# Row sums of the 8-wide squares on TensorE at places 4, 13 and 14 of a period of sixteen

## The chip, the cores and the metric

The kernel runs on one core of one Trainium2 chip. The metric is the device time of one execution in microseconds. The engines are named as in the profile: PE (TensorE, with PEld for its weight loads), DVE (VectorE), ACT (ScalarE), POOL (GpSimd) and SP (SyncE, which here only issues DMAs). Each engine works through its own queue of instructions in order, and the order of PE, DVE, ACT and POOL is fixed when the kernel is written.

## The reference

The input x has 8 batches of 512 tokens of 256 numbers. Four layers follow each other, each added to x after a layer norm: attention A, a feed-forward block, attention B, and the same feed-forward block again. Attention A is the unusual one. It projects each token to 16 heads of 64 channels, and attends *between the channels of one head of one token*:

```
Q = (x @ Wq + bq).reshape(b, s, 16, 64) / 8        # K and V alike, without the 1/8
scores = einsum('bshq,bshk->bshqk', Q, K)          # 64 x 64 for each token and head
w = softmax(where(k > q, -inf, scores))            # causal in the channels
out = x + einsum('bshqk,bshk->bshq', w, V).reshape(b, s, 1024) @ Wo + bo
```

For each q this needs two row sums over k <= q: of exp(q k), the denominator, and of exp(q k) v, the numerator. The feed-forward block has two gate products, two hidden layers of 1024 x 1024 and an output product. Attention B is an ordinary causal attention over 512 tokens with 16 heads.

## The kernel before

**Tiles.** Attention A works on tiles of 128 tokens (the partitions) and 4 heads (256 columns). Batch b has 16 such tiles: group g of heads (0 to 3, the outer loop) and token tile i (0 to 3). Tile number n = 16b + 4g + i, and *the place* of a tile is n mod 16; sixteen tiles make a period. So place 4 is g = 1, i = 0; place 13 is g = 3, i = 1; place 14 is g = 3, i = 2.

**Squares.** The triangle k < q of a head is cut into one square of 32, two of 16, four of 8, and so on down to 1; the diagonal is added apart (`acc`, line 834). Each square is an outer product of rows q and columns k, and its row sums are wanted. A tile has four units (`units`): unit 0 and unit 2 (the 32-squares of two heads each), unit 1 (the 16-squares), and unit 3 (all squares of 8, 4, 2 and 1, tile `ws`, two halves of 1920 columns: exp, and exp times v). A unit runs through these steps:

- `scores` (L855): the products q k, units 0 to 2 on POOL in two instructions each, unit 3 on DVE in four;
- `exps` (L878) on ACT;
- `weigh` (L890): times v, on DVE;
- `halve` (L897), units 0 to 2: a DMA issued by POOL adds one half of `w` to the other in place (accumulate, 1 MB);
- the sums of what is left. Unit 0 by PE: `sums32` (L918) turns 16 blocks of 128 columns into one accumulating PSUM block, `keep_sums` (L980, ACT) copies it, `turn_sums` (L989, PE) turns it back, `add32` (L1000, DVE) adds it to `acc`. Unit 2: a POOL add (`fold`, L905) and a DVE reduction; unit 1: a DVE reduction. Unit 3: `gather` (L1047) reduces the squares of 8 and of 4 on DVE into `red` tiles, `small_squares` (L1023, L1063) does those of 2 and 1 on POOL, and `adds` (L1063) adds the `red` tiles to `acc` on POOL;
- `invert` (L1069, DVE), `divide` (L1075, POOL), `turn_group` (L1085, PE), `keep_att` (L1089, ACT), `project_out` (L1101, PE) and `new_x` (L1114, ACT) finish the tile.

The PSUM tile `bank` has two halves. Half 1 serves only `sums32` (first 128 columns) and `turn_sums` (the other 128); half 0 serves the projections of a tile (L803), the turned x (L621), `turn_group` and `project_out`. `take` and `free` check when the kernel is built that no two uses overlap.

**Order.** A tile has a new slot every 1/12 of a tile period. The table `order` gives each step a slot relative to its tile (step `gather 3` at slot 18 of tile n stands in the same slot as step 6 of tile n + 1), and `slot()` (line 741) issues what falls on a slot in the table's own order. The first batch has a table of its own (`first`). Attention A of batch b runs beside the later layers of batch b - 1, which are written as one generator (`after_a`):

```
while spent * 12 * NT * NG < total * (at + 1 - 12 * NT * NG - 33):
    spent += next(done)
```

Each step of that generator is worth some units (`pace` times a number), and `total` is the worth of one batch. So the hidden layers (L1365 on PE, L1326 and L1327 on ACT, L1331 on DVE), the gate (L1293 on PE, L1268 and L1276 on ACT, L1272 and L1277 on DVE) and attention B (L1444, L1511, L1523) stand at fixed places between the steps of attention A: in batch 3 the hidden layers of one feed-forward block run between the reciprocals of places 2 and 6, attention B between those of 6 and 11, the gate of the other block between those of 11 and 13, and its hidden layers from there to the end of the period.

Of the kernel before, what the change touches and what calls it, by code (L numbers as in the profile page):

```python
# [9 lines left out]
F32 = mybir.dt.float32  # L10
# [33 lines left out]
 'p16': 2,  # L44
 'rot': 4,
 'half': [0, 0, 0, 0, 1, 1],
 'order': [[8, 'scores', 2, 1, 2], [10, 'exps', 2], [22, 'small_squares'], [20, 'add16'], [-120, 'load'],
           [-26, 'normalise'], [6, 'exps', 1], [13, 'sums32', 0], [23, 'adds', 3], [32, 'turn_group'],
           [22, 'keep_sums', 2], [16, 'keep16'], [9, 'weigh', 1], [-1, 'scores', 0, 0, 2], [11, 'fold', 0],
           [12, 'turn16'], [6, 'halve', 0], [11, 'scores', 3, 0, 1], [-30, 'ahead'], [14, 'sums16'],  # L50
           [22, 'add32', 2], [12, 'weigh', 2], [21, 'turn_sums', 2], [34, 'project_out'],
           [4, 'scores', 1, 1, 2], [-8, 'project'], [10, 'halve', 1], [36, 'new_x'], [25, 'divide'],
           [13, 'weigh', 3], [7, 'scores', 2, 0, 2], [15, 'turn_sums', 0], [17, 'fold', 2], [32, 'keep_att'],
           [-5, 'keep_qk'], [12, 'halve', 2], [13, 'keep_sums', 0], [18, 'add32', 0], [18, 'gather', 3],
           [-22, 'turn_x'], [24, 'invert'], [13, 'gather', 1], [16, 'adds', 1], [20, 'sums32', 2],
           [12, 'exps', 3], [4, 'weigh', 0], [3, 'exps', 0], [1, 'scores', 1, 0, 2], [-22, 'keep_x'],
           [0, 'scores', 0, 1, 2]],
 'first': {'sum': ['pe16', 'pe16'],
           'p16': 2,
           'sum16': 'dve',  # L60
           'order': [[21, 'small_squares'], [23, 'adds', 3], [21, 'sums32', 2], [-23, 'turn_x'],
                     [29, 'divide'], [0, 'scores', 0, 1, 2], [4, 'scores', 1, 0, 2], [15, 'turn16'],
                     [26, 'invert'], [19, 'add32', 0], [6, 'scores', 2, 0, 2], [6, 'halve', 0],
                     [-1, 'scores', 0, 0, 2], [-27, 'normalise'], [9, 'fold', 0], [7, 'exps', 1],
                     [10, 'exps', 2], [20, 'gather', 3], [15, 'turn_sums', 0], [4, 'weigh', 0],
                     [23, 'turn_sums', 2], [15, 'weigh', 3], [-120, 'load'], [-30, 'ahead'], [16, 'keep16'],
                     [10, 'scores', 3, 0, 1], [-21, 'keep_x'], [17, 'adds', 1], [19, 'sums16'],
                     [23, 'add32', 2], [8, 'weigh', 1], [10, 'halve', 1], [36, 'new_x'],
                     [4, 'scores', 1, 1, 2], [13, 'weigh', 2], [-5, 'keep_qk'], [6, 'scores', 2, 1, 2],
                     [14, 'exps', 3], [31, 'turn_group'], [21, 'add16'], [21, 'keep_sums', 2],  # L70
                     [15, 'gather', 1], [32, 'keep_att'], [13, 'fold', 2], [14, 'sums32', 0],
                     [14, 'keep_sums', 0], [-8, 'project'], [34, 'project_out'], [13, 'halve', 2],
                     [2, 'exps', 0]],
           'on': ['adds0']},
 'sum16': 'dve',
 'lo': 'psum',
 'pace': {'gate': 1.8, 'attn': 0.65, 'wait': 1.354, 'w3': 1.05, 'out': 0.95, 'turn': 0.997},
 'total': 304.842,
 'eps': 'dve',
 'U': {'wait': 14.4,  # L80
       'gate': 33.0,
# [3 lines left out]
       'out': 5.6,  # L85
       'qk': 13.6,
       'attn': 72,
       'proj': 21}}


@with_exitstack
# [241 lines left out]
def fast_path(ctx: ExitStack, tc: tile.TileContext, k, t, flag):  # L333
# [216 lines left out]
    def bank_half(j):  # L550
        return bank[:, j, :]
# [85 lines left out]

    JB = 8

    def kind(b, n_u):  # L640
        c = G["first"] if b == 0 and "first" in G else G
        return c["sum"][n_u // 2] if n_u in (0, 2) else c.get("sum16", "dve")

    def reds(b):
        return (G["first"] if b == 0 and "first" in G else G).get("red", [])

    def on(b):
        return (G["first"] if b == 0 and "first" in G else G).get("on", [])

    def p16(b):  # L650
        return (G["first"] if b == 0 and "first" in G else G)["p16"]

    def by_columns(b, n_u):
        return n_u < 3 and kind(b, n_u) != "dve"
# [1 line left out]
    def pieces(w, n, off, nsq, cols, b, n_u, parts):  # L656
# [4 lines left out]
        def of_cols(v):  # L661
            return v[:, cols].rearrange("p (x t) -> p x t", t=2 * n)[:, :, :n]

        if n < 16:
            e, ev = (
                w[:, a * SMALL + off : a * SMALL + off + nsq * n * n].rearrange("p (x i j) -> p x i j", i=n, j=n)
                for a in range(2)
            )
            yield e, ev, lambda v: of_rows(v).unsqueeze(3), lambda v: of_cols(v).unsqueeze(2)
        elif by_columns(b, n_u):  # L670
            both = w.rearrange("p (j a x i) -> p a j x i", a=2, x=nsq, i=n)
            step = n // parts
            for k in range(0, n, step):
                yield (
                    both[:, 0, k : k + step],
                    both[:, 1, k : k + step],
                    lambda v: of_rows(v).unsqueeze(1),
                    lambda v, k=k: of_cols(v)[:, :, k : k + step].rearrange("p x j -> p j x").unsqueeze(3),
                )
        elif n == 32:  # L680
            both = w.rearrange("p (b a x i j) -> p a b x i j", a=2, x=nsq, i=n, j=JB)
            for x in range(nsq):
                yield (
                    both[:, 0, :, x],
                    both[:, 1, :, x],
                    lambda v, x=x: of_rows(v)[:, x].unsqueeze(1).unsqueeze(3),
                    lambda v, x=x: of_cols(v)[:, x].rearrange("p (b j) -> p b j", j=JB).unsqueeze(2),
                )
        else:
            both = w.rearrange("p (b a x i j) -> p a b x i j", a=2, x=nsq, i=n, j=JB)  # L690
            for k in range(n // JB):
                yield (
                    both[:, 0, k],
                    both[:, 1, k],
                    lambda v: of_rows(v).unsqueeze(3),
                    lambda v, k=k: of_cols(v)[:, :, k * JB : (k + 1) * JB].unsqueeze(2),
                )
# [10 lines left out]
    class AttentionA:  # L708
# [32 lines left out]
        def slot(self, t):  # L741

            now = []
            for lo, hi, order in TABLES:
                for place, (slot, what, args) in enumerate(order):
                    late = 8 if what in ("normalise", "turn_x", "keep_x") and t - slot in (12, 20) else 0
                    n, r = divmod(t - slot - late, 12)
                    if r == 0 and lo <= n < hi and (late == 0 or t - slot == 20):
                        now.append((place / len(order), what, self.todo[n] + args))
            for _, what, args in sorted(now, key=lambda p: p[0]):  # L750
                getattr(self, what)(*args)

        def take(self, h, *cells):
# [175 lines left out]
        def sums16(self, b, i, g):  # L929
# [1 line left out]
            if kind(b, 1) == "dve": return  # L931
            assert (b, i, g, 1, "h") in self.seen
            w = self.live.pop((b, i, g, 1)).rearrange("p (j r) -> p j r", r=2 * P)
            self.take(1, 0, 1)
            for r in range(2):
                for j in range(8):
                    nc.tensor.matmul(
                        bank_half(1)[:, r * P : (r + 1) * P], w[:, j, r * P : (r + 1) * P], ident,
                        start=(j == 0 and r == 0), stop=(j == 7), is_transpose=True, skip_group_check=True,
                    )  # L940
            assert "fwd" not in self.live
# [2 lines left out]
        def keep16(self, b, i, g):  # L944
# [1 line left out]
            if kind(b, 1) == "dve": return  # L946
            assert self.live.pop("fwd") == (b, i, g, 1)
            self.live["sums16"] = ap_.tile([P, 2 * P], F32, tag="red128", name="sums16", bufs=3)
            nc.scalar.copy(self.live["sums16"], bank_half(1))
            self.free(1, 0, 1)  # L950

        def turn16(self, b, i, g):

# [1 line left out]
            assert "back" not in self.live  # L955
            self.live["back"] = (b, i, g, 1)
            s16 = self.live.pop("sums16")
            self.take(1, 0, 1)
            for r in range(2):
                nc.tensor.transpose(bank_half(1)[:, r * P : (r + 1) * P], s16[:, r * P : (r + 1) * P], ident)  # L960

        def add16(self, b, i, g):

            if kind(b, 1) == "dve": return
# [1 line left out]
            acc = self.live[b, i, g][2]  # L966
            rows = acc.rearrange("p a (x t) -> p a x t", t=32)[..., 16:]
            nc.vector.tensor_tensor(
                rows, rows, bank_half(1).rearrange("p (a x i) -> p a x i", a=2, i=16), ALU.add
            )  # L970
            assert (b, i, g, 0, "w") in self.seen
            self.free(1, 0, 1)
            self.done[b, i, g] += 1

        def keep_sums(self, b, i, g, n_u):
# [38 lines left out]
        def small_squares(self, b, i, g):  # L1014
# [4 lines left out]
            for n, off, nsq, cols in squares(units[NU - 1]):  # L1019
                if n <= 2 and n not in reds(b):  # L1020
# [1 line left out]
                    if n == 2:  # L1022
                        (nc.vector if "small" in on(b) else nc.gpsimd).tensor_tensor(both[..., :1], both[..., :1], both[..., 1:], ALU.add)  # L1023
                    self.add_rows(b, i, g, n, cols, both[..., 0], "small")
            if (b, i, g, NU - 1, "r") in self.seen: self.live.pop((b, i, g, NU - 1))

        def gather(self, b, i, g, n_u):

# [1 line left out]
            assert (b, i, g, n_u, "h" if n_u < NU - 1 else "w") in self.seen  # L1030
            self.seen.add((b, i, g, n_u, "r"))
            w = self.live[b, i, g, n_u]
            if n_u < NU - 1 or (b, i, g, n_u, "s") in self.seen: self.live.pop((b, i, g, n_u))
            self.sums[b, i, g, n_u] = []
            here = 0
            for n, off, nsq, cols in sorted(squares(units[n_u]), key=lambda u: u[0] in reds(b)):
                if n in reds(b):
                    assert all((b, i, g, k, what) in self.seen for k in range(NU) for what in "pew")
                    red = self.live[b, i, g][0][:, here % 2].rearrange("p (a r) -> p a r", a=2)
# [719 lines left out]
```

## Time and profile before

| | us |
|---|---|
| three runs | 3621.72, 3622.65, 3628.54 (median 3622.65) |
| the profiled execution | 3620.43, of which the span of its instructions is 3618.6 |
| DVE busy | 3124.0 (86%) |
| PE busy | 3048.9 (84%) |
| POOL busy | 2971.8 (82%) |
| ACT busy | 2505.2 (69%) |
| first and last reciprocal of attention A (L1069) | at 53.2 and 3328.6 |

A reciprocal ends the sums of a tile, so its 128 starts mark the tiles. Batch 0, which runs alone, takes 337.9 us from its first reciprocal to that of batch 1; the six periods after it take 422.8, 422.0, 420.1, 425.0, 426.6 and 424.3 us; after the last reciprocal 290 us follow in which the later layers of batch 7 run alone. A row of a group of instructions reads: line, engine, operation, tiles and shapes, count | busy us, mean ns of one | idle time of the engine just before them, and what ended it. In the timeline the number in square brackets is the idle time of the engine before that instruction and what released it. A row of a window reads: stretch, its length, then PE, PEld, DVE, ACT and POOL busy us with counts, the clock granted to PE (1.00 is full), the DMA share and GB/s.

### The profile page before, as it was taken

The page shows a single profiled execution, that of the slowest core. Times are in us where ns is not written, and L with a number is a line of the kernel's source. Part 1 is how long each engine was busy: PE and PEld are TensorE (multiplying, and loading weights), DVE is VectorE, ACT ScalarE, POOL GpSimd, SP SyncE. Part 2 cuts the span into 40 slices and gives each one's busy share as a digit, 9 for nine tenths or more (in the row PEclk, how much of TensorE's full clock was granted, in tenths as well). Part 3 has the DMA queues.
Part 4 walks back from the last instruction along what each step waited for, and adds up shares of the span by engine and source line. Part 5 has one row for each costly group of instructions (what it writes and reads, how often), then busy time and mean ns, then how long its engine had stood idle before and what let it go on. Part 6 is the DMA issues. An engine that isn't in the chain of part 4 may idle for free.

```text
span 3618.6 us, 42449 instructions
## 1 busy us (share of the span) xinstructions
PE 3048.9 (84%) x14468; PEld 2168.6 (60%) x14468; DVE 3124.0 (86%) x3844; ACT 2505.2 (69%) x3488; POOL 2971.8 (82%) x2682
## 2 busy tenths in 40 slices
PE   7765698798887998888987988879888889878998
PEld 4544475476645766466754766457664667556756
DVE  7999998999889998999988998899989998896227
ACT  4544686687767787687866877668866878665453
POOL 7999988888898989989898888989889888885000
PEclk8878799898998999998998989989999999989999
DMA  9978897688877988689876888769877788767414
GB/s 240 200 160 165 178 228 163 149 215 194 206 165 167 231 206 185 141 204 213 224 167 144 217 191 204 167 155 232 195 190 150 193 208 209 175 146 221 131 53 170
DMA packets 117038, 665.34 MB, mean 184 GB/s; under 512 B 12742, under 2 KB 30665, under 8 KB 43467
## 3 DMA queue, kind: packets, MB, share of 16 engines
q0 software_dynamic: 80640, 587.24, 71.1%
q1 hardware_dynamic: 35896, 75.02, 6.0%
q8 instruction: 116, 1.90, 0.2%
q14 instruction: 110, 0.90, 0.1%
q10 hardware_dynamic: 276, 0.27, 0.0%
HBM read 251.18 MB, written 8.65 MB: 72 GB/s over the span
## 4 chain that ended last, share of the span: by engine, by line
PE 33%; DVE 22%; POOL 17%; ACT 14%; issue 9%; DMA 5%; ACTq 0%; POOLq 0%; SPq 0%; DVEq 0%
POOL w L855 8%; PE ph L1365 8%; DVE w L890 6%; DVE red L1047 5%; DMA w<-w 5%; PE pw L1293 4%; POOL acc L1063 3%; PE pyb L1523 3%; ACT w L878 3%; DVE ws L855 3%; PE pqkb L1444 3%; PE bank L918 3%; PE psb L1511 2%; POOL w L897 2%; PE qv L808 2%
## 5 line engine op out<-in xcount | busy, mean ns | idle before, releaser
L855 POOL TENSOR_TENSOR w<-k 128x1024 f32<-128x1024 f32 x768 | 1617.6, 2194 | 44.2 <-DVE red L1047 23.0
L1365 PE MATMUL ph<-h,hidden 128*128 128x512 f32 x4096 | 1019.6, 403 | 6.5 <-DVE h L1277 2.4
L890 DVE TENSOR_TENSOR w<-w,qv 128x1024 f32<-128x1024 f32 (+1 forms) x624 | 890.2, 1458 | 83.9 <-ACT w L878 83.8
L1365 PEld LDWEIGHTS ph<-h,hidden 128*128 128x128 f32 x4096 | 766.4, 190 | 186.7 <-issue 21.0
L878 ACT ACTIVATE w<-w 128x2048 f32<-128x2048 f32 x384 | 734.6, 1915 | 138.5 <-POOL w L855 136.5
L897 POOL DMA_DIRECT2D w<-w x384 | 352.3, 918 | 193.3 <-DVE w L890 94.7
L1293 PE MATMUL pw<-xnt,gate 128*128 128x512 f32 (+2 forms) x1152 | 346.4, 452 | 153.4 <-ACT silu L1268 99.3
L1047 DVE TENSOR_REDUCE red<-w 128x256 f32<-128x2048 f32 x240 | 426.8, 1778 | 23.7 <-DMA w<-w 22.0
L1047 DVE TENSOR_REDUCE red<-ws 128x256 f32<-128x2048 f32 (+1 forms) x256 | 435.6, 1742 | 0.0
L1063 POOL TENSOR_TENSOR acc<-acc,red 128x256 f32<-128x256 f32 x496 | 392.1, 791 | 29.5 <-DVE red L1047 11.0
L1293 PEld LDWEIGHTS pw<-xnt,gate 128*128 128x128 f32 x1152 | 236.3, 225 | 242.1 <-ACT silu L1268 124.0
L918 PE MATMUL bank<-ident,w 128*128 128x128 f32 x2304 | 322.6, 301 | 52.1 <-ACT x L1114 26.4
L855 DVE TENSOR_TENSOR ws<-qv,k 128x1024 f32<-128x1024 f32 (+3 forms) x512 | 300.0, 647 | 76.9 <-POOL acc L1063 76.8
L918 PEld LDWEIGHTS bank<-ident,w 128*128 128x128 f32 x2304 | 298.3, 158 | 80.0 <-ACT x L1114 39.2
L890 DVE TENSOR_TENSOR ws<-ws,qv 128x1024 f32<-128x1024 f32 (+3 forms) x512 | 294.9, 636 | 32.0 <-ACT ws L878 32.0
L905 POOL TENSOR_TENSOR w<-w 128x1024 f32<-128x1024 f32 x112 | 280.2, 2502 | 50.7 <-DMA w<-w 50.6
L808 PE MATMUL qv<-wqv,xnta 128*128 128x512 f32 x512 | 269.9, 653 | 27.3 <-DVE ws L890 22.0
L878 ACT ACTIVATE ws<-ws 128x1920 f32<-128x1920 f32 x128 | 233.1, 1821 | 76.2 <-DVE ws L855 72.6
L1331 DVE TENSOR_TENSOR h<-ph,h 128x512 fp32r<-128x512 f32 x256 | 167.8, 681 | 90.3 <-ACT ph L1327 84.1
L1518 ACT ACTIVATE eb<-psb 128x512 f32<-128x512 f32 (+3 forms) x503 | 181.9, 459 | 89.2 <-PE psb L1515 88.9
L1326 ACT ACTIVATE h<-ph,s_sb 128x512 fp32r<-128x512 f32 x256 | 176.6, 690 | 94.2 <-PE ph L1365 92.2
L1069 DVE RECIPROCAL acc<-acc 128x256 f32<-128x256 f32 x128 | 223.1, 1743 | 3.9 <-POOL acc L1063 3.9
(163 smaller groups left out, 4867.5 us busy)
## 6 DMA issues: line engine op xcount, KB each, us to landing
w<-w POOLq DMA_DIRECT2D x384, 1024.0 KB, 7.6
hidden<-in_h POOLq DMA_DIRECT2D x128, 1024.0 KB, 6.4
gate<-in_w12p POOLq DMA_DIRECT2D x32, 1024.0 KB, 6.7
w<-in_w3p POOLq DMA_DIRECT2D x16, 1024.0 KB, 6.0
wqv<-wqv_d SPq DMA_DIRECT2D x31, 512.0 KB, 3.9
wo<-in_wo SPq DMA_DIRECT2D x32, 256.0 KB, 7.4
w<-in_h SPq DMA_DIRECT2D x8, 1024.0 KB, 6.9
wk<-wk_d SPq DMA_DIRECT2D x31, 256.0 KB, 6.2
```

Of the source, the lines that this page charges most:

```text
L808: nc.tensor.matmul(qv.rearrange("p j f -> p (j f)"), xnt[:, c, :], wqv[:, c, :], start=(c == 0), stop=(c == DC - 1),)
L855: eng.tensor_tensor(e, rows(q).to_broadcast(shape), columns(kt[:, 0]).to_broadcast(shape), ALU.mult)
L878: nc.scalar.activation(e, e, AF.Exp, scale=C**-0.5)
L890: nc.vector.tensor_tensor(ev, e, columns(qv[:, 1]).to_broadcast(list(e.shape)), ALU.mult)
L897: nc.gpsimd.dma_start(w[:, :2048], w[:, 2048:], accum_op=ALU.add)
L905: nc.gpsimd.tensor_tensor(w[:, :1024], w[:, :1024], w[:, 1024:2048], ALU.add)
L918: nc.tensor.matmul(bank_half(G["half"][4])[:, :P], w[:, j * P : (j + 1) * P], ident, start=(j == 0), stop=(j == n - 1), is_transpose=True,)
L1047: nc.vector.tensor_reduce(red, self.columns_of(w, n, off, nsq), AX.X, ALU.add)
L1063: (nc.vector if what == "psum" or what in on(b) else nc.gpsimd).tensor_tensor(rows, rows, part.rearrange("p a (x i) -> p a x i", i=n), ALU ...
L1069: nc.vector.reciprocal(acc[:, 0, :], acc[:, 0, :])
L1293: nc.tensor.matmul(pj[:, toks], w[:, m % 4, j, c, :], xs[:, p, c, toks], start=(p == 0 and c == 0), stop=(p == 1 and c == DC - 1),)
L1365: nc.tensor.matmul(pss[j], w[:, j, c, :], h_in(p, c), start=(p == 0 and c == 0), stop=(p == 1 and c == MC - 1),)
```

## The change

Three places get another way to sum the squares of 8. The rest of the diff is knobs that keep their old value (`half16`, `half8`) and the layout.

```
- 'pace': {... 'wait': 1.354, ...},   'total': 304.842,
+ 'pace': {... 'wait': 1.422, ...},   'total': 305.821,
+ 'kinds': {'3': {}, '4': {'sum8': 'pe'}, '13': {'sum8': 'pe'}, '14': {'sum8': 'pe'}, '0': {}}
...
+    def kinds(b):
+        if b == 0 and "first" in G:
+            return G["first"]
+        return {**G, **G.get("kinds", {}).get(str(place[0]), {})}
...
-        if n < 16:
+        if n == 8 and kind8(b) == "pe":
+            e, ev = (
+                w[:, a * SMALL + off : a * SMALL + off + nsq * n * n].rearrange("p (j x i) -> p j x i", j=n, i=n)
+                for a in range(2)
+            )
+            yield e, ev, lambda v: of_rows(v).unsqueeze(1), lambda v: of_cols(v).rearrange("p x j -> p j x").unsqueeze(3)
+        elif n < 16:
...
+        def sums8(self, b, i, g):
...
+            self.take(h, 0, 1)
+            for r in range(2):
+                for j in range(8):
+                    nc.tensor.matmul(
+                        bank_half(h)[:, r * P : (r + 1) * P], w[:, r * SMALL + j * P : r * SMALL + (j + 1) * P], ident,
+                        start=(j == 0 and r == 0), stop=(j == 7), is_transpose=True, skip_group_check=True,
+                    )
+        def keep8(self, b, i, g):
...
+            nc.scalar.copy(self.live["sums8"], bank_half(h))
+        def turn8(self, b, i, g):
...
+            for r in range(2):
+                nc.tensor.transpose(bank_half(h)[:, r * P : (r + 1) * P], s8[:, r * P : (r + 1) * P], ident)
+        def add8(self, b, i, g):
...
+            nc.vector.tensor_tensor(
+                rows, rows, bank_half(h).rearrange("p (a x i) -> p a x i", a=2, i=8), ALU.add
+            )
...
             for n, off, nsq, cols in sorted(squares(units[n_u]), key=lambda u: u[0] in reds(b)):
+                if n == 8 and kind8(b) == "pe": continue
```

Batch 0 returns its own table, so the new way is taken at three places of batches 1 to 7, 21 tiles. There the squares of 8 lie in `ws` with the column j outermost, so that eight blocks of 128 columns are to be added; `sums8` (slot 18, behind `add32` of unit 0 in the same slot) does that on PE in half 1 of `bank`, 16 transposes; `keep8` (slot 19) copies 256 columns on ACT; `turn8` (slot 20) turns them back, two transposes; `add8` (slot 23, between unit 3's `scores` and unit 2's `weigh` of the next tile) adds them to `acc` on DVE. The reduction of the squares of 8 on DVE and their add on POOL are not issued.

The table `order` is written anew. Most of it is the same order with other tie breaks; the slots that differ for steps that are issued are `scores 1, 1` (the second product of unit 1 on POOL, from 4 to 1), `divide` (25 to 27) and `keep_att` (32 to 33). Set beside each other, the two kernels' queues differ thus. PE has 378 more instructions (21 x 18), ACT 21 more, POOL 21 fewer, DVE as many as before. In batch 0 only the three copies of the turned x of batch 1 and one DMA issue change places. In batches 1 to 7, POOL issues `halve 1` ahead of the add of unit 2's sums (a `red` of 128 columns), not behind it, and does `divide` behind both products of unit 1, not ahead of or between them. ACT has `keep_att` some steps later at some tiles. Where the second feed-forward block starts, around place 13, one `silu`, one layer-norm step, one split of the gate (L1277) and one projection trade places with a neighbour. SP's queue issues the same DMAs in the same order. Against the reciprocals, the products of the later layers stand where they stood, to within a step, and behind the last reciprocal PE has the same number of instructions as before.

## The prediction

> **What bounds the kernel.** I read the page's first part, then the stretches between reciprocals (period of batch 3), then the waits of the seven periods, then the timeline around the three places.
>
> ```profile
> PE 3048.9 (84%) x14468; PEld 2168.6 (60%) x14468; DVE 3124.0 (86%) x3844; ACT 2505.2 (69%) x3488; POOL 2971.8 (82%) x2682
> ```
>
> No engine is full over the span, so the tiles have different limits. The stretches that hold the changed steps, and the ones behind them, are these (place 3 to 4, 4 to 5, 12 to 13, 13 to 14, 14 to 15):
>
> ```profile
> 1316.60:1341.20 24.60, 24.46 (x108) 18.94 (x107) 24.13 (x29) 23.87 (x28) 23.60 (x21) 1.00 0.88 209
> 1341.20:1368.90 27.70, 26.93 (x132) 21.67 (x132) 23.15 (x26) 19.39 (x23) 23.08 (x21) 1.00 0.98 261
> ...
> 1547.70:1581.00 33.30, 24.27 (x100) 18.01 (x101) 28.69 (x36) 25.43 (x31) 22.88 (x20) 0.86 0.69 162
> 1581.00:1605.40 24.40, 23.99 (x111) 19.14 (x110) 23.45 (x27) 20.32 (x25) 22.37 (x21) 1.00 0.92 232
> 1605.40:1630.10 24.70, 22.48 (x98) 17.45 (x97) 22.94 (x26) 22.14 (x29) 24.35 (x21) 0.93 0.92 218
> ```
>
> Before place 4, PE, DVE, ACT and POOL are all within 1 us of full. Behind it PE has 0.8 us free of 27.7. Before place 13, DVE has most (28.69 of 33.30) and PE 9 us free. Around place 14 PE has 0.4 us free, then 2.2. The waits say how the engines are tied together:
>
> ```profile
> POOL w L897 <- DVE w L890: 90.8, 46, 3.4
> DVE w L890 <- ACT w L878: 76.0, 62, 3.1
> DVE ws L855 <- POOL acc L1063: 68.9, 49, 3.6
> DVE red L1047 <- DMA w<-w: 17.7, 14, 4.2
> ```
>
> The third is a loop of one tile: unit 3's `scores` on DVE needs `ws` free, which POOL frees with `small_squares`; `weigh 2` follows on DVE, and POOL's `halve 2` waits for that before its next products. Where DVE waits for POOL there, DVE time saved in the same tile is worth nothing.
>
> **Prices.**
>
> ```profile
> L887 DVE TENSOR_TENSOR acc<-acc,qv 128x256 f32<-128x256 f32 x128 | 52.4, 409 | 29.4 <-ACT acc L869 29.1
> L1047 DVE TENSOR_REDUCE red<-ws 128x256 f32<-128x2048 f32 x128 | 291.4, 2277 | 0.0
> L1063 POOL TENSOR_TENSOR acc<-acc,red 128x256 f32<-128x256 f32 x384 | 340.8, 888 | 18.2 <-DVE red L1047 8.1
> ...
> 1553.73 1.76 PE bank L918 x16
> ...
> 1571.62 0.44 PE bank L1085 x2
> 1572.09 0.38 ACT att L1089
> ```
>
> Each of the 21 tiles loses a DVE reduction (2.28 us) and a POOL add (0.89), and gains an `add8` on DVE of the form of L887 (one operand in PSUM, 0.41), 16 transposes on PE (1.76, from the chain of waits) and two (0.44), and an ACT copy (0.38). So DVE -1.87, POOL -0.89, PE +2.20, ACT +0.38: over 21 tiles -39, -19, +46, +8 us. Neither -39 nor +46 is the answer; each place decides. The new layout of `ws` costs nothing: DVE's products of 1024 columns take 1.21 us in the 16-squares and 1.22 in `ws`, which lie differently.
>
> The Trainium skill (TensorE: Matmul & The Clock Gate, "Wait — 56ns, not 53.3ns?") measures back-to-back matmuls of 128 columns at 55.6 ns at the full clock and 106.7 at half. By it 18 transposes would take about 1.0 us at a granted 1.00, an estimate, and a PE cost of 21 us instead of 46. Here 16 took 1.76 us, 110 ns each, and 1.75 where the granted clock was 1.00, so the row decides.
>
> **Place 13: -1.4 us a period** (bounds -1.87 and 0). The place where `sums8` goes lies between two gate products, where PE is idle:
>
> ```profile
> 1569.08 2.54 PE L1293 MATMUL pw<-xnt,gate 128*128 128x512 f32 x8 [3.11 <-DVE h L1277]
> ```
>
> 3.11 us cover the 1.76. What PE waits for is DVE, which stands in the two `ws` reductions (1565.03 to 1568.43) and has no gap from there to the next `ws` product at 1576.44; POOL's `small_squares` had ended at 1571.05, 5.4 us earlier. So the 2.28 us come off a busy DVE; the gate's product behind (L1272, at 1571.33) then meets its silu (done 1569.51), which leaves about 1.8 us; `add8` gives back 0.41. POOL's `halve 2`, 2.3 us early here, follows DVE. If the gate's chain on ACT binds instead, the gain is 0.
>
> **Place 14: -0.7** (bounds -0.89 and +1.8). DVE gains nothing: it waits 0.77 us for POOL's `small_squares` at its next `ws` product (1600.89). POOL decides:
>
> ```profile
> 1606.87 0.89 POOL L897 DMA_DIRECT2D w<-w  x1
> ...
> 1620.76 0.44 PE L1085 MATMUL bank<-ident,acc 128*128 128x128 f32 x2 [2.06 <-ACT k L823]
> ...
> 1625.59 2.35 DVE L855 TENSOR_TENSOR ws<-qv,k 128x1024 f32<-128x1024 f32 x4 [1.33 <-POOL acc L1063]
> ```
>
> `halve 2` starts at 1606.87 with no wait before it, 1.4 us after its `weigh` ended (1605.50), and one tile later DVE waits 1.33 us for POOL again. So the missing POOL add comes off the loop, and `add8` lies in the 1.4 us. PE's 2.20 us make it late until 1620.76, where it had 2.06 us free; ACT's `sums` (1608.78) came 1.7 us after its transposes ended. I take 0.2 off for the rest. `keep8` stalls ACT: ACT gets there at 1593.4, `sums8` ends near 1594.7, and behind it stand the copies of `k`, `att` (which idled 1.10) and the Gelus that DVE's L1331 needs; the 0.77 covers most of it. Without these covers it costs 2.20 less the 0.4 free, +1.8.
>
> **Place 4: +0.7** (bounds -0.3 and +2.2). PE is saturated from `sums8` (about 1327) to the next unit 0's transposes, and ACT already waits for those:
>
> ```profile
> 1344.62 0.27 ACT L980 COPY sums<-bank 128x128 f32<-128x128 f32 x1 [3.73 <-PE bank L918]
> ...
> 1352.16 2.29 DVE L890 TENSOR_TENSOR w<-w,qv 128x2048 f32<-128x2048 f32 x1 [1.38 <-ACT w L878]
> ...
> 1364.38 2.35 DVE L855 TENSOR_TENSOR ws<-qv,k 128x1024 f32<-128x1024 f32 x4 [1.50 <-POOL acc L1063]
> ```
>
> Behind `sums` on ACT stand two Gelus and the exps of unit 0, for which DVE waits 1.38. So PE's 2.20 us reach DVE at 1352, and 1.50 of them vanish in its wait for POOL at 1364: +0.7. DVE's saving is lost to ACT, since L1331 already waits there for the Gelus (0.47), and POOL's to a DMA that lands late.
>
> `sums8` itself waits for `add32`, which frees half 1; behind it stand all of PE's products. `add32` ends at 1326.7 and PE gets there at 1327.2, 0.5 us later; at place 13 the lead is 0.9 us and at 14 it is 1.3: no stall.
>
> **The layout: -0.3 a period** (bounds -0.9 and +3.0). `halve 1` now goes out ahead of a POOL add of 0.46 (128 columns, L1063). The gain is at most that at the 14 waits for a landed DMA, -0.9 a period. The loss is at most 0.46 at the 46 waits of POOL for `weigh`, +3.0, but nearly each tile has a second wait, at `halve 2`, that takes it up. `divide` behind unit 1's products makes those 1.0 us earlier for ACT; `turn_group` came 10 us after `divide`. The moved rows at the gate I price at nothing either way, under the idle PE there.
>
> **Sum.** -1.4 - 0.7 + 0.7 - 0.3 = -1.7 a period, seven periods: -12 us. Batch 0 and the 290 us behind the last reciprocal stay. 3620.4 - 12 = 3608.4 for an execution like the profiled one; the median stood 2.2 above it, so **3611 us**, 0.3% faster.
>
> **Rivals.** About 0.2%, 7 us, is what a measurement of this kernel can tell from no change.
>
> - *PE becomes the bound* (slower). In the two stretches from place 3 to 6 PE has 2.2 us free in 76.8, from 13 to the period's end 2.6 in 75.0, just what is added. If those gaps are waits that can't be filled, places 4 and 14 cost 2.20 each; with -1.4 at place 13 that is +3.0 a period, +21: 3644. It decides once PE's free time there falls under 2.2 us. For it: the 24.46 of 24.60. Against it: the 2.06 us at 1620.76. Chance 0.25.
> - *The saving is given back*: place 13's gain ends in POOL's loop at 14, whose waits are no shorter, and 4 pays for 14: near 3622, within 3615 to 3629. For it: 49 waits of DVE for POOL. Chance 0.28.
> - *DVE bounds everywhere*: all -39 us and the layout's -2 land: 3582. Against it: the waits at 1600.89 and 1364.38. Chance 0.09.
> - *The forecast*, 3600 to 3615: 0.38.
>
> The change does do what it says: the queues show the transposes. Faster 0.47, within 0.2% 0.28, slower 0.25. The range 3590 to 3642 leaves out most of the third rival and the far half of the first, about 0.2.
>
> **What would show it.** In the changed profile: L1047 on `ws` of 2048 columns 107 times; 336 transposes of `ws` at near 110 ns; in the stretch before place 13's reciprocal PE's idle time of 3.1 us gone and the stretch about 1.5 us shorter; ACT's wait for `sums` behind place 4 grown from 3.7 to near 6; the stretch from 14 to 15 shorter by the POOL add. A wait of DVE's for ACT behind place 14 that was not there, or a longer stretch 13 to 14, would prove it wrong, and so would a batch 0 that changes.

## The result, and the profile after

The changed kernel takes 3641.49 us (median of 5 runs, 3637.84 to 3646.42), beside 3623.92 for the kernel before on the same chip: ratio 1.0047, 95% interval 1.0033 to 1.0062. It is slower by 17.6 us; the forecast was 3611. The profiled execution took 3643.51 us, its span 3641.4. Busy times from the first part of its page:

```profile
PE 3084.1 (85%) x14846; PEld 2216.5 (61%) x14846; DVE 3087.6 (85%) x3844; ACT 2509.1 (69%) x3509; POOL 2950.9 (81%) x2661
```

The work moved much as priced: DVE -36.4 (forecast -39), POOL -20.9 (-19), PE +35.2 (+46), ACT +3.9 (+8). So the engines do what was said, and the loss must be in waits. Batch 0 (first reciprocal at 52.9, that of batch 1 at 391.1) and the 291 us behind the last reciprocal are as before; all but 1 us of the loss lies in the seven periods.

The stretches of batch 3 that the prediction showed, in the changed kernel (place 3 to 4, 4 to 5, 12 to 13, 13 to 14, 14 to 15; columns as there):

```profile
1316.50:1343.00 26.50, 26.50 (x127) 21.11 (x126) 22.39 (x29) 24.19 (x29) 23.17 (x21) 1.00 0.91 209
1343.00:1368.80 25.80, 25.05 (x121) 19.98 (x120) 22.95 (x26) 19.36 (x23) 22.59 (x20) 1.00 1.00 269
...
1547.20:1579.80 32.60, 26.59 (x115) 20.76 (x116) 26.94 (x35) 25.77 (x32) 22.12 (x19) 0.83 0.68 162
1579.80:1605.10 25.30, 24.89 (x125) 20.26 (x124) 21.91 (x27) 20.46 (x26) 23.20 (x20) 1.00 0.94 235
1605.10:1629.80 24.70, 22.62 (x100) 17.82 (x100) 23.02 (x26) 21.24 (x27) 22.98 (x20) 0.93 0.86 205
```

Before, these took 24.60, 27.70, 33.30, 24.40 and 24.70. Place 4 adds 1.9 and gives 1.9 back, place 13 brings 0.7, the stretch behind it loses 0.9: nothing of 17 us is to be found here. Two stretches with *no* changed sum in them hold the loss. From place 8 to 9 in batch 5, first before, then after:

```profile
2298.30:2320.90 22.60, 19.40 (x145) 9.23 (x143) 20.52 (x22) 18.20 (x37) 21.57 (x18) 1.00 0.78 172
```

```profile
2303.20:2331.10 27.90, 22.57 (x185) 11.15 (x177) 20.83 (x23) 19.65 (x42) 21.94 (x18) 1.00 0.66 144
```

This is attention B. The stretch is 5.3 us longer, with the same work on DVE and POOL; PE and ACT have 3.2 and 1.5 us more in it, which came late from the stretch before. PE is idle for 5.3 of the 27.9 us at a full clock: every engine waits. Over all seven periods, the mean change of a stretch (us, place k to k + 1, differences of reciprocals' starts; the others are within 0.4):

| kernel | 3 | 4 | 8 | 9 | 12 | 13 |
|---|---|---|---|---|---|---|
| changed | +2.3 | -3.0 | **+2.2** | **+1.9** | -0.9 | +0.7 |

Stretches 8 and 9 together are 4.1 us a period, 29 us in all; the rest of the seven periods is 7 us better than before.

The waits of the seven periods. First the four that the prediction showed, as they are now, then those that tell of the loss:

```profile
POOL w L913 <- DVE w L906: 119.2, 59, 4.8
DVE w L906 <- ACT w L894: 96.5, 75, 3.5
DVE ws L871 <- POOL acc L1129: 43.6, 45, 3.1
DVE red L1113 <- DMA w<-w: 14.7, 14, 3.2
...
ACT eb L1584 <- PE psb L1581: 118.9, 71, 4.9
POOL w L871 <- PE bank L934: 43.1, 24, 4.4
PE bank L1151 <- ACT k L839: 46.9, 31, 4.0
PE bank L1167 <- ACT att L1155: 27.0, 20, 2.3
```

The last four in the kernel before:

```profile
ACT eb L1518 <- PE psb L1515: 84.9, 65, 3.4
POOL w L855 <- PE bank L918: 11.1, 11, 1.6
PE bank L1085 <- ACT k L823: 36.8, 24, 4.0
PE bank L1101 <- ACT att L1089: 8.6, 13, 2.1
```

Of the first four, the waits of DVE and POOL along the chain from ACT to POOL grew, and DVE's wait for POOL fell from 68.9 to 43.6, the loop that place 14 was to relieve. Of the last four all grew: PE stands in `project_out` for the copy `att` (8.6 to 27.0) and in `turn_group` for the copy of k (36.8 to 46.9), ACT's attention B exps (`eb`) wait for PE's scores (84.9 to 118.9), and POOL waits for PE (11.1 to 43.1).

### The profile page after: what moved, and what is told of

Its sections match the earlier page's. It is cut to its first block, busy times and chain, and to the rows that moved or that the text cites. A ratio compares the mean times of both kernels' runs of the same rounds, so it can differ in the third digit from the quotient of the medians.

```text
span 3641.4 us, 43159 instructions
## 1 busy us (share of the span) xinstructions
PE 3084.1 (85%) x14846; PEld 2216.5 (61%) x14846; DVE 3087.6 (85%) x3844; ACT 2509.1 (69%) x3509; POOL 2950.9 (81%) x2661
## 4 chain that ended last, share of the span: by engine, by line
PE 51%; DVE 17%; ACT 14%; POOL 10%; issue 5%; DMA 3%; ACTq 0%; POOLq 0%; DVEq 0%
PE ph L1431 19%; POOL w L871 6%; DVE w L906 4%; DVE red L1113 4%; PE bank L934 4%; PE pyb L1589 4%; PE pw L1359 4%; ACT w L894 3%; PE qv L824 3%; PE psb L1577 3%; DMA w<-w 3%; PE pqkb L1510 2%; PE bank L1167 2%; ACT eb L1584 2%; POOL acc L1129 2%
## 5 line engine op out<-in xcount | busy, mean ns | idle before, releaser
L871 POOL TENSOR_TENSOR w<-k 128x1024 f32<-128x1024 f32 x768 | 1579.9, 2179 | 81.3 <-PE bank L934 51.5
L1129 POOL TENSOR_TENSOR acc<-acc,red 128x256 f32<-128x256 f32 (+1 forms) x475 | 375.5, 790 | 23.5 <-DVE red L1113 7.2
L1113 DVE TENSOR_REDUCE red<-ws 128x256 f32<-128x2048 f32 (+1 forms) x235 | 389.7, 1696 | 0.0
```

The costliest lines, as they stand in the source:

```text
L871: eng.tensor_tensor(e, rows(q).to_broadcast(shape), columns(kt[:, 0]).to_broadcast(shape), ALU.mult)
L1113: nc.vector.tensor_reduce(red, self.columns_of(w, n, off, nsq), AX.X, ALU.add)
L1129: (nc.vector if what == "psum" or what in on(b) else nc.gpsimd).tensor_tensor(rows, rows, part.rearrange("p a (x i) -> p a x i", i=n), ALU ...
```

## The experiments

The theory formed from these waits: the copy `keep_att`, moved from slot 32 to 33, falls on ACT behind the four exps of an attention B group; PE, which is in `project_out`, waits for it, and the scores for the next exps are queued behind `project_out` on PE. Rivals: PE's 2.2 us bound at the three places; POOL's new order; the new pace. "Ratio" is to the kernel before on the same chip (medians 3624.29, 3624.79, 3622.89 and 3621.62 in the four groups of four). It can differ from the quotient of the two medians, here by 0.0012 at most.

| run | us | ratio, 95% interval |
|---|---|---|
| `sums_alone` | 3622.74 | 0.9996, 0.9983 to 1.0009 |
| `layout_alone` | 3651.20 | 1.0071, 1.0050 to 1.0093 |
| `att_back` | 3620.39 | 0.9993, 0.9977 to 1.0008 |
| `pool_back` | 3648.49 | 1.0057, 1.0037 to 1.0077 |
| `att_late` | 3629.85 | 1.0016, 1.0004 to 1.0028 |
| `out35` | 3640.08 | 1.0052, 1.0034 to 1.0070 |
| `s13` | 3607.44 | 0.9945, 0.9929 to 0.9962 |
| `s14` | 3627.14 | 1.0008, 0.9995 to 1.0022 |
| `att_pace` | 3651.54 | 1.0080, 1.0067 to 1.0094 |
| `pace_back` | 3629.94 | 1.0020, 1.0009 to 1.0030 |
| `s4` | 3616.76 | 0.9983, 0.9972 to 0.9995 |
| `lay13` | 3616.19 | 0.9981, 0.9967 to 0.9994 |
| `s13_14` | 3621.48 | 1.0000, 0.9988 to 1.0011 |
| `s4_13` | 3606.80 | 0.9950, 0.9937 to 0.9964 |
| `s4_14` | 3630.52 | 1.0021, 1.0010 to 1.0031 |
| `s13_pace` | 3616.49 | 0.9974, 0.9961 to 0.9987 |

**The two halves of the change.** `sums_alone` puts the new sums into the old order, `layout_alone` has the new order with no new sum:

```
sums_alone, on the kernel before:
+ [18, 'sums8'] behind [18, 'add32', 0];  [19, 'keep8'] first;  [20, 'turn8'] behind [20, 'sums32', 2]
+ [23, 'add8'] behind [11, 'scores', 3, 0, 1];  'kinds': 4, 13, 14: {'sum8': 'pe'}
layout_alone, on the changed kernel:
- 'kinds': {'3': {}, '4': {'sum8': 'pe'}, '13': ..., '14': ..., '0': {}}
+ 'kinds': {}
```

> The order and pace of the kernel before, and in it the new sums at places 4, 13 and 14 (16 and 2 transposes, the copy and the add put in at their slots, nothing else moved). In the changed kernel the stretches around places 3 to 6 and 12 to 16 sum to about -1 us a period and those from 8 to 10 to +4. If the layout is the cause of the loss, this kernel has the first without the second: 3616 us, 0.1 to 0.3% under the kernel before. If the added work on TensorE is the cause, it is as slow as the changed kernel: 3641.

> The changed kernel with the new sums taken out at all places: its order and pace alone. If the layout is the cause, it is slower than the kernel before by the 28 us of the stretches from 8 to 10 (seven times 4.1) less what little it may gain elsewhere: 3640 to 3652, and these stretches read as in the changed kernel. If the added work on TensorE is the cause, it is within 0.2% of the kernel before: 3617 to 3631.

The sums by themselves change nothing that can be measured; the layout by itself costs 0.71% (27 us by the medians), at least the whole loss: the two intervals overlap. So PE's added work is not what makes the kernel slower.

**Which part of the layout.**

```
att_back, on the changed kernel:    - [33, 'keep_att']             + [32, 'keep_att']
pool_back, on the changed kernel:   - [1, 'scores', 1, 1, 2]       + [4, 'scores', 1, 1, 2]
                                    - [27, 'divide']               + [25, 'divide']
att_late, on the kernel before:     - [32, 'keep_att']             + [33, 'keep_att']
out35, on the changed kernel:       - [34, 'project_out']          + [35, 'project_out']
```

> The changed kernel with the copy of the turned tile (keep_att) at slot 32 again, where it was before; only ACT's queue differs, the copy alone moves. Theory of the late copy: at slot 33 it stands behind a group of attention B's exps in ACT's queue, and the output projection in front of the next scores in TensorE's queue waits for it; then this kernel loses the 4 us a period of stretches 8 to 10 and reads near 3616. Rival, POOL's order or the pace: no change, 3637 to 3646.

> The changed kernel with the second product of unit 1 at slot 4 and the division at slot 25 again; only POOL's queue differs. Theory of POOL's order: with the division behind unit 1's products, POOL waits idle for the buffer that TensorE's transposes free (81 us of idle before these products, against 44), and has no division to fill it; then this kernel wins back most of the loss: 3615 to 3625. Theory of the late copy: at most the 37 us of wait move to another place, 3634 to 3646.

> The kernel before with one number changed: the copy of the turned tile (keep_att) at slot 33, not 32; only ACT's queue differs, and no sums move to TensorE. If the late copy alone makes the layout's loss, this is as slow as the layout alone, 1.007 of the kernel before: 3643 to 3655, with TensorE's wait for that copy near 27 us (8.6 before) and ACT's wait for attention B's scores near 119 (85 before). If it takes POOL's new order as well, it stays within 0.2% of the kernel before.

> The changed kernel, its copy left at slot 33, with the output projection of the tile (project_out) at slot 35, not 34; only TensorE's queue differs. If the harm is that TensorE stands in project_out waiting for the copy while attention B's scores queue behind it, this undoes it as the earlier copy did: 3616 to 3628, TensorE's wait for the copy under 10 us. If the late copy harms through ACT's own queue, it stays at 3637 to 3646.

With one number put back (`att_back`, where only ACT's queue differs from the changed kernel's) the loss is gone: 1.0047 becomes 0.9993, and the waits of the seven periods return:

```profile
ACT eb L1584 <- PE psb L1581: 88.3, 70, 3.4
POOL w L871 <- PE bank L934: 18.2, 14, 2.4
PE bank L1151 <- ACT k L839: 48.3, 31, 4.0
PE bank L1167 <- ACT att L1155: 5.6, 10, 1.6
```

Three of the four are near what they were before; the third is not, which comes up below. `pool_back` stays slow, so these two moves on POOL are not the cause; POOL's third, `halve 1` ahead of the add, stays as changed in `pool_back` and in `att_back`, and in `att_back` nothing is lost with it. `out35` lets PE go on to attention B and come to `project_out` a slot later. It removes the loss where the theory puts it (stretch 8 +0.8, stretch 9 -0.6, PE's wait for `att` 2.8), and shows that PE's place in its queue is the link. But the kernel isn't faster. The wait that grew is that of ACT for the end of the tile:

```profile
ACT x L1180 <- PE bank L535: 90.0, 39, 4.7
```

It was 30.7 before. 26.0 of the 90.0 us lie in stretch 12, where there was no such wait, and stretch 12 grows by 2.5; what the rest costs was not taken apart. And `att_late` is the miss that matters: the same late copy on the old order costs 0.16%, not 0.7%. The copy alone is not enough.

**Copy and pace.** On ACT the late copy falls behind four exps of attention B at 11 tiles with the old pace (place 8 in batches 2 to 7, place 9 in 4 to 7, place 7 in 7), and at 14 with the new one (place 8 in 1 to 7, place 9 in 4 to 7, place 7 in 5 to 7). On PE, the new pace sets `turn_group` or `project_out` of place 7, in batches 4 to 6, ahead of 20 products of attention B (a group's 8 value products, 8 scores and 4 masks). At place 8 of batch 1 `turn_group` moves likewise, and at place 6 of batches 1 and 2 `project_out` moves ahead of 8 of its projections.

```
att_pace, on the kernel before:     - [32, 'keep_att']             + [33, 'keep_att']
                                    - 'wait': 1.354                + 'wait': 1.422
                                    - 'total': 304.842             + 'total': 305.821
pace_back, on the changed kernel:   - 'wait': 1.422                + 'wait': 1.354
                                    - 'total': 305.821             + 'total': 304.842
```

> The kernel before, with two knobs of the change only: the copy of att at slot 33 and the new pace of the later layers (wait 1.422, total 305.821). No sum of squares is moved; PE's and DVE's queues are then those of the layout alone. Theory (the pace shifts attention B by a step or so against the slots, so that with the new pace the late copy falls behind four exps of attention B at 14 tiles instead of 11, and the two knobs together make the layout's loss): near the layout alone, 3645 to 3652 us (+0.55% to +0.75%), stretches 8 and 9 longer by about 2 us each in every period, PE's wait for att in project_out near 27 us. Rival (the loss needs POOL's or ACT's other moves of the layout as well): near the late copy on the old order, 3628 to 3634 us.

> The changed kernel with the old pace (wait 1.354, total 304.842), all else as changed, the late copy of att too. Theory (late copy times pace): most of the loss goes, 3626 to 3632 us (+0.05% to +0.2%), since the late copy then costs what it costs on the old order; stretch 9 stays about 2 us longer, stretch 8 gets back to within 1 us of before. Rival (the pace is harmless, the order of the new table does it): it stays at 3638 to 3645 us.

Both came where the theory put them. Two knobs make the whole loss, and the stretches show where (us a period; they come from one profiled execution each, so they are read for places and not for totals: those of `sums_alone` and `att_back` took 3631 and 3630 us, above their medians):

| pace | copy | kernels | stretch 8 | stretch 9 |
|---|---|---|---|---|
| old | slot 33 | `att_late`, `pace_back` | +0.5, +0.5 | +2.7, +2.6 |
| new | slot 32 | `att_back`, `s13_pace`, `lay13` | +0.9, +0.8, +1.0 | -0.5, -0.5, -0.6 |
| new | slot 33 | changed, `att_pace`, `layout_alone` | +2.2, +2.0, +1.9 | +1.9, +2.3, +2.4 |

The times need both knobs, and the stretches don't show all of the reason. With the late copy and the old pace, stretches 8 and 9 are already 3.2 us a period longer, 23 us in all, and the time of `att_late` is only 5 us longer: in its profiled execution the other stretches are 12 us shorter than before, spread over the period. In that of `att_pace` they are 6 us longer. What gives the time back with the old pace, and why the new pace takes that away, is not shown.

PE's queue in the changed kernel, batch 5, from place 7 to 9 (start, us, instruction, idle time before it and what ended it):

```profile
2292.77 0.69 PE L1151 MATMUL bank<-ident,acc 128*128 128x128 f32 x2 [4.04 <-ACT k L839]
...
2295.25 1.66 PE L1577 MATMUL psb<-qkb,qkb 32*128 32x384 f32 x8
...
2299.19 2.07 PE L1167 MATMUL bank<-wo,att 128*128 128x256 f32 x4 [1.73 <-ACT att L1155]
...
2327.03 1.13 PE L1167 MATMUL bank<-wo,att 128*128 128x256 f32 x4 [2.31 <-ACT att L1155]
```

And ACT's:

```profile
2297.23 1.64 ACT L1584 ACTIVATE eb<-psb 128x384 f32<-128x384 f32 x4 [4.24 <-PE psb L1581]
2298.73 0.41 ACT L1155 COPY att<-bank 128x256 f32<-128x256 f32 x1
...
2324.64 2.06 ACT L1584 ACTIVATE eb<-psb 128x512 f32<-128x512 f32 x4 [0.71 <-PE psb L1581]
2326.57 0.41 ACT L1155 COPY att<-bank 128x256 f32<-128x256 f32 x1
...
2330.70 1.64 ACT L1584 ACTIVATE eb<-psb 128x384 f32<-128x384 f32 x4 [1.93 <-PE psb L1581]
```

Read the two together. Place 7: `turn_group` stands ahead of the scores of the 384 group (the pace) and waits 4.04 us for the copy of k; those scores come late, the exps wait 4.24 for them; the copy `att` stands behind these exps (the late slot), and `project_out` waits 1.73 more with the next scores behind it. Place 8: the copy stands behind the 512 exps, `project_out` waits 2.31, the next exps 1.93.

Some of the lateness at place 7 is PE's clock. Behind the 4.04 us the clock granted to PE is 0.50 from 2293 to 2302 (1.00 over the same microseconds with the old pace), and the 384 group's scores take 1.66 us and `project_out` 2.07, where they take 0.93 and 1.08 in the next view. This belongs to the pace's share: `att_back` has the same wait of 4.04 and the same half clock there, and its stretch 8 of batch 5 is longer by 2.7 us, that of the changed kernel by 5.2.

With the old pace and the same late copy (`pace_back`), PE has:

```profile
2293.55 0.93 PE L1577 MATMUL psb<-qkb,qkb 32*128 32x384 f32 x8
...
2294.65 0.42 PE L1151 MATMUL bank<-ident,acc 128*128 128x128 f32 x2
...
2298.10 1.08 PE L1167 MATMUL bank<-wo,att 128*128 128x256 f32 x4
...
2321.83 1.22 PE L1167 MATMUL bank<-wo,att 128*128 128x256 f32 x4 [2.31 <-ACT att L1155]
```

The scores go first, `project_out` of place 7 waits for nothing, and only that of place 8 does. The pace's own mark is PE's wait for k in `turn_group`: 34.5 to 37.4 us in the kernels with the old pace (before, `att_late`, `pace_back`, `s13`, `s4`), 44.2 to 50.6 in those with the new (changed, `layout_alone`, `att_pace`, `att_back`, `out35`, `lay13`, `s13_pace`).

**The places one by one**, all on the old order with the early copy, edits as `sums_alone` but for `kinds`; `lay13` is the changed kernel with `keep_att` at 32 and place 13 alone, `s13_pace` is `s13` with the new `wait` and `total`:

```
s13, s14, s4:             'kinds': {'13': {'sum8': 'pe'}}, or '14', or '4'
s13_14, s4_13, s4_14:     the same in pairs
lay13:                    [32, 'keep_att'], 'kinds': {'13': {'sum8': 'pe'}}
s13_pace:                 s13 with 'wait': 1.422, 'total': 305.821
```

> The order before, with the new sums at place 13 alone. All three places together gained 1.4 us in the stretch behind place 12 and lost 1.6 in the next. If that loss is place 14's own, place 13 alone keeps its gain as the prediction had it: -1.4 us a period, 3614, no longer stretch 13. If the gain of place 13 is given back at the next tile whatever that does, stretch 13 grows by 1 us or more here too, and the time is 3620 to 3627.

> The order before, with the new sums at place 14 alone. If the 1.6 us that the three places together lost in stretch 13 are place 14's own (ACT stalled by keep8, TensorE's 2.2 us), they are seen here as well, and the time is 3628 to 3636. If they are place 13's gain given back, stretch 13 keeps its 24.5 us, and the prediction's -0.7 a period gives 3619.

> The kernel before with the squares of 8 summed on PE at place 4 alone, 7 tiles, on the old order with the copy of att at slot 32. By the prediction's step +0.7 us a period, 3629 us. By the three places together on the old order (stretch 3 to 4 longer by 1.9, 4 to 5 shorter by 1.8, about 0 in all) 3622 to 3626 us. A rival by which what place 13 gains was lost at place 4 and not at 14 wants 3632 us or more.

> The changed kernel with the copy of att back at slot 32 and the new sum at place 13 alone: the new pace and the new order, 7 tiles. If the rest of the layout (pace, POOL's order, divide) is worth nothing by itself, as the run with only the copy put back suggests, it comes within 0.2% of place 13 alone on the old order, 3600 to 3614 us. If the rest of the layout brings the 0.3 us a period that the prediction gave it, 3598 to 3607 us. If the rest costs time that the other places hid, 3615 us or more.

> The kernel before with the new sum at places 13 and 14 on the old order, 14 tiles. Theory (place 14's stall of ACT in its copy of the sums sits in the stretch behind place 13 and takes back what place 13 gained): 3616 to 3624 us, near no change, with stretch 12 to 13 shorter by 1.2 to 1.4 and 13 to 14 longer by 1.6. Rival (the two add up, -0.55% and +0.08%): 3602 to 3610 us.

> The kernel before with the new sum at places 4 and 13 on the old order, 14 tiles. If the two add up (-0.17% and -0.55%): 3594 to 3604 us, the fastest so far. If place 4 takes back part of place 13's gain a period later: 3608 to 3618 us.

> The kernel before with the new sum at places 4 and 14 on the old order, 14 tiles. If the two add up (-0.17% and +0.08%): 3617 to 3623 us. If they take from each other, since place 4 of the next period follows place 14 in a chain that has no free time between: 3626 us or more.

> Place 13 alone on the old order, with the new pace of the later layers (wait 1.422, total 305.821) and the copy of att early. If the new pace costs the gain by itself (stretch 8 to 9 longer by about 0.9 in the runs with the new pace and the early copy): 3613 to 3620 us, like the layout with place 13 alone. If the order on POOL and ACT costs it: 3603 to 3610 us, like place 13 alone.

| kernel | stretch 3 | 4 | 12 | 13 |
|---|---|---|---|---|
| `s13` | +0.2 | -0.4 | -1.2 | 0.0 |
| `s14` | -0.1 | -0.5 | +0.2 | +1.7 |
| `s4` | +1.8 | -1.9 | 0.0 | 0.0 |
| `s13_14` | 0.0 | +0.3 | -1.2 | +1.3 |
| `s4_13` | +2.0 | -1.9 | -1.2 | 0.0 |
| `s4_14` | +1.9 | -1.9 | +0.2 | +1.5 |
| `sums_alone` | +1.9 | -1.8 | -1.4 | +1.6 |

Each place keeps its mark in whatever company. Place 13 brings 1.2 to 1.4 us, place 14 costs 1.3 to 1.7, place 4 moves 1.9 us from one stretch to the next. With place 14, every kernel loses what the others gain (`s13_14` 1.0000, `sums_alone` 0.9996), so it is there that place 13's gain goes. The times do not add, though. Place 14 costs 0.08% alone, 0.55% beside place 13 (`s13_14` and `s13`) and 0.38% beside place 4 (`s4_14` and `s4`), while its mark of 1.3 to 1.7 us a period is worth 0.25 to 0.33%; why is not shown. `s13` and `s4_13` beat both kernels, by 0.55% and 0.50% against before. `s4` came out better than expected from the three together, and 4 with 13 is no better than 13 alone: the two intervals overlap, so whether place 4's 0.17% is kept stays open. The new pace costs place 13 half its gain even with the early copy (`s13_pace` 0.9974, `lay13` 0.9981). Stretch 8's +0.8 to +1.0 is a part of that, but stretch 9 gives 0.5 to 0.6 back, so the rest is not located; what the other moved steps of the layout add lies within the intervals.

Place 13 in `s13`, on DVE in batch 3:

```profile
1571.44 0.28 DVE L1016 TENSOR_TENSOR acc<-acc,bank 128x128 f32<-128x128 f32 x1
1571.63 1.21 DVE L1113 TENSOR_REDUCE red<-ws 128x256 f32<-128x1024 f32 x1
...
1576.15 0.76 DVE L1338 SCALAR_TENSOR_TENSOR pw<-pw,s_sb,silu 128x512 f32<-128x512 f32 x1 [0.32 <-ACT silu L1334]
...
1583.52 0.41 DVE L1085 TENSOR_TENSOR acc<-acc,bank 128x256 f32<-128x256 f32 x1
...
1586.11 1.74 DVE L1135 RECIPROCAL acc<-acc 128x256 f32<-128x256 f32 x1
```

The same in the kernel before:

```profile
1564.83 0.28 DVE L1000 TENSOR_TENSOR acc<-acc,bank 128x128 f32<-128x128 f32 x1
1565.03 3.40 DVE L1047 TENSOR_REDUCE red<-ws 128x256 f32<-128x2048 f32 x2
...
1580.96 1.74 DVE L1069 RECIPROCAL acc<-acc 128x256 f32<-128x256 f32 x1
```

From `add32` to the reciprocal DVE takes 14.67 us, not 16.13: the reduction (3.40 to 1.21) comes off a full engine, `add8` (0.33 to the next start) and a wait of 0.32 for the silu go back on it.

Place 14 in `s14`, batch 3, ACT and then DVE:

```profile
1599.49 0.38 ACT L1069 COPY sums<-bank 128x256 f32<-128x256 f32 x1 [2.34 <-PE bank L1058]
...
1601.55 0.37 ACT L1155 COPY att<-bank 128x256 f32<-128x256 f32 x1 [1.13 <-PE bank L1151]
...
1603.23 0.69 ACT L1392 ACTIVATE h<-ph,s_sb 128x512 fp32r<-128x512 f32 x1
```

```profile
1584.63 1.75 DVE L1135 RECIPROCAL acc<-acc 128x256 f32<-128x256 f32 x1
...
1598.05 2.34 DVE L906 TENSOR_TENSOR w<-w,qv 128x1024 f32<-128x1024 f32 x2
1604.51 0.69 DVE L1397 TENSOR_TENSOR h<-ph,h 128x512 fp32r<-128x512 f32 x1 [4.12 <-ACT ph L1393]
```

Before, the same Gelu on ACT and the same two instructions on DVE:

```profile
1596.67 0.69 ACT L1326 ACTIVATE h<-ph,s_sb 128x512 fp32r<-128x512 f32 x1
```

```profile
1595.98 2.33 DVE L890 TENSOR_TENSOR w<-w,qv 128x1024 f32<-128x1024 f32 x2
1598.23 0.68 DVE L1331 TENSOR_TENSOR h<-ph,h 128x512 fp32r<-128x512 f32 x1
```

`keep8` holds ACT for 2.34 us (1.57 on the mean of the 7 tiles, 11.0 us in all) until `sums8` is done. Behind it stand the copies of k and `att`, and the Gelus: 18.60 us after the reciprocal, 15.71 before (1603.23 - 1584.63; 1596.67 - 1580.96). DVE, which saved its 2.19, comes earlier and waits 4.12 for them. In the changed kernel the same two waits are 1.60 and 1.74 at this tile, and stretch 13 loses 0.7. No run has a later slot for `keep8`, so the stall as the cause is read from these rows and not tested.

## Why the prediction was wrong

- **The layout, -0.3 a period: this step failed.** Measured +3.8 (26.9 us over seven periods, `layout_alone`; its interval is 2.6 to 4.8), beside bounds of -0.9 and +3.0. The step priced POOL's `halve 1` and `divide`, which `att_back` (with both, no loss) and `pool_back` (without the second, no gain) show to matter little, and gave the late copy no price at all: that ACT has `keep_att` "some steps later at some tiles" was read off the queues and left there. The question that the prediction asked of `keep8` (what is queued behind the waiting instruction, and who waits for it) was not asked of it. It also took the later layers as standing where they stood "to within a step"; one step of the pace put `turn_group` ahead of a group of scores. What the runs show in its place: the late copy and the new pace together cost 0.80% on the kernel before (`att_pace`), the late copy alone 0.16%.
- **Place 14, -0.7: the second failed step**, "the 0.77 covers most of it". DVE gains nothing, as it said, and ACT's stall was put at 1.3 us (1594.7 less 1593.4) and measured at 1.57. But the cover was taken from DVE's wait for POOL, which lies *behind* the Gelus; ahead of them DVE had no wait to give, and its saved 2.19 us only brought it there earlier. Stretch 13 measured +1.3 to +1.7, near the bound of +1.8, and stretch 14, which was to get shorter by the POOL add, changed by -0.2 in `s14` and +0.4 in the changed kernel. That ACT's stall is the whole cause is read from the rows and not tested by a run.
- **Place 13, -1.4: right**, in mechanism and size: -1.2 to -1.4 in stretch 12 on the old order, -0.9 in the changed kernel. That `s13` gains 17 us and not the 8 to 10 of that stretch is not explained; its stretch 15 is 0.7 shorter, the rest is spread.
- **Place 4, +0.7:** -0.9 by the times of `s4` (6.1 us over seven periods), 0 by stretches 3 and 4 (-0.1, and -0.8 in stretch 5). PE does bind there (26.50 of 26.50 us in the changed kernel, +1.9), but all of the 2.2 us vanish in the next stretch's waits, not 1.5 of them. ACT's wait for `sums` did not grow from 3.7 to 6; it was 3.23.
- **The rivals.** The time landed near "PE becomes the bound" (3644), and the mechanism was another: places 3 to 6 of the changed kernel are 5 us better over seven periods, 12 to the end is even, and PE idles for a fifth of the stretch that lost most. "The saving is given back" is right for the sums on the old order (0.9996), with a different place of the loss: ACT at place 14, not POOL's loop, whose waits did get shorter.
- **Right besides:** batch 0 and the tail stay, the reduction is issued 107 times, and a longer stretch 13 to 14 was named as what would prove it wrong.
- The row for the transposes held against the figure of 55.6 ns that the Trainium skill gives (TensorE: Matmul & The Clock Gate, "Wait — 56ns, not 53.3ns?"). At place 4 of the changed kernel, in a stretch with a granted clock of 1.00, 16 of them took 1.91 us in the timeline, 119 ns each. The 16 of `sums32` take 1.91 there too in the kernel before (at 1580.12); the 1.76 that the prediction used is the same work in the chain of waits.

## What to carry to other kernels

Price every instruction that a new order moves, the cheapest first to be forgotten: for a copy of 0.4 us ask what now stands ahead of it on its engine, who waits for it, and what is queued behind *that* one. Where two stages share in-order queues, a step of one that waits in the middle of a chain of the other (scores, exps, products) stops the chain on both engines. And time saved on an engine is a gain only where its next wait is not for another engine that the same edit has just made later.

## What the runs showed of the hardware

POOL's add of 128 columns takes 458 ns, and 745 directly behind the issue of a DMA, in all kernels with the new order of POOL:

```profile
L1063 POOL TENSOR_TENSOR acc<-acc,red 128x128 f32<-128x128 f32 x112 | 51.3, 458 | 11.2 <-DVE red L1047 2.9
```

```profile
L1129 POOL TENSOR_TENSOR acc<-acc,red 128x128 f32<-128x128 f32 x112 | 83.5, 745 | 0.1
```

The adds of 256 columns fell from 888 to 804 ns at the same time, 32 us up and 30 down (363 x 0.084), so POOL as a whole is not slower. These too are longer directly behind a DMA issue, 1.01 to 1.02 us on the mean against 0.79 to 0.83 elsewhere, and 121 of them stood there before, 29 in the changed kernel. So the span that POOL's profile shows for an add goes with what was issued ahead of it.

The 16 transposes of `sums8` in the changed kernel took 1.91 us in batch 3 at places 4 and 14 and 2.43 at place 13. Behind PE's wait of 2.12 us for the silu there, the clock granted was 0.50 from 1565 to 1568; stretch 12 got shorter all the same.
